# Layer 1's rows of a MetaFormer kernel: 25 depthwise taps split anew over VectorE, GpSimd and TensorE, with VectorE's sums held in PSUM

## The chip, the cores and the metric

The kernel runs as one program on one core of a Trainium2 chip. The metric is the device time of one execution in microseconds (us). Before the change three runs took 8144.84, 8158.97 and 8159.37 us; the median is 8158.97.

## The reference

Two MetaFormer layers are applied to an input of 2 images x 96 channels x 96 x 96 pixels. The change lies in the last stage of layer 1. What is computed there:

```python
lepe = lax.conv_general_dilated(v.reshape(B, C, H, W), lepe_w, (1, 1), [(pad, pad), (pad, pad)],
    dimension_numbers=('NCHW', 'OIHW', 'NCHW'), feature_group_count=C)      # 5 x 5, one filter per channel
...
dmat = jax.nn.softmax(dmat, axis=-1)               # each pixel against the 3 x 3 cells near it
feature = jnp.einsum('bnpk,bckn->bnpc', dmat, feat_unfold)
out = feature.reshape(B, hh, ww, R, R, C).transpose(0, 5, 1, 3, 2, 4).reshape(B, C, H, W)
out = out + lepe
out = jnp.einsum('oc,bchw->bohw', proj_w, out) + proj_b[None, :, None, None]
...
x = x + _L1_conv_ref(_ln_c(x), ...)
t = t + _L1_ffn_ref(_ln_t(t), ...)                 # LayerNorm, 96 -> 384 -> 96 with fp8 rounding of inputs
```

`lepe` is the part concerned: for every channel the values `v` are multiplied by 25 weights at 25 shifts ("taps") and summed.

## The kernel before

Layer 0 runs first, for both images. Layer 1 then runs image by image in three stages: `_l1_before` (normalise, keys and queries), `_l1_attention` (the result is `dist`, one vector per cell of 2 x 2 pixels), and the stage `rows`, which finishes the layer. Only `rows` is touched. It works on strips of R = 12 image rows, eight for each image, called q0 to q7 here. `_l1_turn` first turns `dist` round on TensorE. Then `_l1_rows` records for each strip:

- `values(g)`, four times: TensorE multiplies four rows of the input by `W.v` (L1694), ScalarE copies the result from PSUM into `vch` (L1697), a tile of 96 channels x 16 rows x 100 columns in fp32: the strip's 12 rows with two rows and columns around them. Small GpSimd memsets (L1681 and on) clear the edge. `vch` has three buffers.
- `near(i)`, three times: scores `st` on TensorE, exponentials `e` on ScalarE, the sums `pd` and `po` on TensorE, the inverse `rd` by Ln and Exp on ScalarE, and the product `ft` on VectorE (L1747).
- the taps. Four of the 25 (`ON_PE`) are left to TensorE. VectorE does the other 21 over the whole strip, 1152 elements of each of 96 partitions at a time: one multiplication (L1759) and 20 multiply-and-add instructions (L1762) which read `vch` and `acc` and write `acc` again, all in SBUF.
- `project(c2)` for each half of six rows, in two parts `c` of three rows (288 columns) each: TensorE sums in one bank `pp` the four taps with weights `W.pt` (L1778), `ft` times `W.p` (L1782) and, as a step of its own that waits for the taps, `acc` times `W.p` (L1788). VectorE adds bias and residual and gives `x3` (L1791). Then comes the FFN of the half, `_plan_ffn`: norm (`fxc` and `fva` on TensorE, square, Ln and Exp on ScalarE, `fxq` on VectorE, L894), `fph` on TensorE, on ScalarE six casts (L909), three Relu (L913) and three conversions to fp8 (L916) into `fh`, `fpy` on TensorE, `fy` on ScalarE (L927, L931), and the residual add on GpSimd (L932). SP issues the loads of `xn` and `xr` and the store of the half.

Single-bank PSUM tiles come from a pool `p` of eight banks.

The order in each engine's queue is not that of the code. Operations are recorded with an engine, an estimated cost, what they read and write, and a due time (`_dues`, from the last argument of `_l1_rows`; here 40 for each strip and 80 from a strip's first operation to its last). `_Plan.order` then lists them: at each step it takes an operation that can start earliest by its own estimates, the due time deciding among those ready at once, and a tile takes a buffer only when one is free. The order so found is fixed: on the chip each engine takes its queue strictly in turn, and where an operation has to wait, everything behind it in that queue waits.

Of the kernel before, what the change touches and what calls it, by code (L numbers as in the profile page):

```python
# [14 lines left out]
ALU = mybir.AluOpType  # L15
# [11 lines left out]
C = 96  # L27
HW = 96
# [5 lines left out]
H2 = T // 2  # L34
# [813 lines left out]
def _dues(S, n0, at):  # L848

    ops = S.ops[n0:]  # L850
    whole, sofar = sum(o.cost for o in ops), 0.0
    for o in ops:
        o.due = at(sofar / whole)
        sofar += o.cost
# [796 lines left out]


NEAR = 2 * (CELLS + 2)
ON_PE = tuple(range(4))


def _l1_rows(k, P, S, W, ffn, M, distT, x2, out, q, at):


    nc = k.nc  # L1660
    n0 = len(S.ops)
    R = 2 * WIN
    op = _op(S)
    ps = lambda name: S.tile(P.ps, [128, 512], "p", 8, name=name)
    temp = lambda name: S.tile(P.wk, [C, T], name, 3)
    xs = S.held(M.xs, "xs")


    vch = S.tile(P.wk, [C, R + 4, HW + 4], "vch", 3)
    y0 = q * R - 2  # L1670

    if q:
        xn = S.tile(P.wk, [C, R + 4, HW], "xn", 2)
        S.op("sp", 1.5, lambda: nc.sync.dma_start(
            xn.ap[:, : min(R + 4, HW - y0)],
            M.xd.rearrange("p (r w) -> p r w", w=HW)[:, y0 : min(y0 + R + 4, HW)]), (), (xn,))
    else:
        xn = S.held(M.xn0, "xn")

    def edges():  # L1680
        nc.gpsimd.memset(vch.ap[:, :, 0:2], 0.0)  # L1681
        nc.gpsimd.memset(vch.ap[:, :, HW + 2 :], 0.0)
        if y0 < 0:
            nc.gpsimd.memset(vch.ap[:, 0:2, :], 0.0)
        if y0 + R + 4 > HW:
            nc.gpsimd.memset(vch.ap[:, R + 2 :, :], 0.0)

    op("pool", 200, edges, (), ((vch, "e"),))

    def values(g):  # L1690
        lo, hi = max(y0 + 4 * g, 0), min(y0 + 4 * g + 4, HW)
        n = (hi - lo) * HW
        pv = ps("pv2")
        op("pe", n, lambda: nc.tensor.matmul(  # L1694
            pv.ap[:C, :n], W.v, xn.ap[:, lo - y0 : hi - y0], start=True, stop=True),
            (xn,), (pv,), (vch,))
        op("act", n, lambda: nc.scalar.copy(  # L1697
            vch.ap[:, lo - y0 : hi - y0, 2 : HW + 2],
            pv.ap[:C, :n].rearrange("p (r w) -> p r w", w=HW)), (pv,), ((vch, g),))

    for g in range(4):
        values(g)

    ft = S.tile(P.wk, [C, 3, 384], "ft", 2)

    def near(i):
        j = 3 * q + i  # L1710
        toks = slice(4 * j - y0, 4 * j - y0 + 4)
        e = [S.tile(P.wk, [NEAR, 384], "e", 4) for _ in range(2)]
        po, pd, rd = ps("po"), ps("pd"), S.tile(P.wk, [C, 384], "rd", 2)
        for t in range(2):
            st = ps("st")

            def part(t=t, st=st):
                def run():
                    nc.tensor.matmul(
                        st.ap[:NEAR, :384],  # L1720
                        xs.ap[:, 2 * j + 2 * t : 2 * j + 2 * t + 2, :].rearrange("p r w -> p (r w)"),
                        xn.ap[:, toks], start=True, stop=False)
                    nc.tensor.matmul(
                        st.ap[:NEAR, :384], W.far, W.mask[:, t], start=False, stop=True)

                op("pe", 480, run, (xs, xn), (st,), (e[t],))
                op("act", 384, lambda: nc.scalar.activation(
                    e[t].ap, st.ap[:NEAR, :384], AF.Exp, scale=C**-0.5), (st,), (e[t],), tab="e")

            part()  # L1730

        def sums(dst, w):
            def run():
                for t in range(2):
                    nc.tensor.matmul(dst.ap[:C, :384], w(t), e[t].ap, start=(t == 0), stop=(t == 1))  # L1735

            op("pe", 768, run, e + [distT], (dst,), (rd, ft))

        sums(pd, lambda t: k.ones[:NEAR])
        sums(po, lambda t: distT.ap[:NEAR, j + t])  # L1740

        def inverse():
            nc.scalar.activation(pd.ap[:C, :384], pd.ap[:C, :384], AF.Ln)
            nc.scalar.activation(rd.ap, pd.ap[:C, :384], AF.Exp, scale=-1.0)

        op("act", 384, inverse, (), (pd, rd), tab="e", times=2)
        op("dve", 384, lambda: nc.vector.tensor_tensor(  # L1747
            ft.ap[:, i], rd.ap, po.ap[:C, :384], ALU.mult), (rd, po), ((ft, i),))

    for i in range(3):  # L1750
        near(i)


    acc = S.tile(P.wk, [C, R, HW], "acc", 2)
    for n, t in enumerate(t for t in range(25) if t not in ON_PE):
        def tap(n=n, t=t):
            src = lambda: vch.ap[:, t // 5 : t // 5 + R, t % 5 : t % 5 + HW]
            if n == 0:
                S.op("dve", 0.9, lambda: nc.vector.tensor_scalar(  # L1759
                    acc.ap, src(), W.lw[:, t : t + 1], None, ALU.mult), (vch,), (acc,))  # L1760
            else:
                S.op("dve", 1.43, lambda: nc.vector.scalar_tensor_tensor(  # L1762
                    acc.ap, src(), W.lw[:, t : t + 1], acc.ap, ALU.mult, ALU.add), (vch,), (acc,))

        tap()

    def project(c2):
        xr, x3 = S.tile(P.wk, [C, T], "xr", 2), temp("x3")
        S.op("sp", 1.0, lambda: nc.sync.dma_start(
            xr.ap, x2[:, (2 * q + c2) * T : (2 * q + c2 + 1) * T]), (), (xr,))  # L1770

        def part(c):
            pp = ps("pp")
            r0, cols = c2 * WIN + 3 * c, slice(c * H2, (c + 1) * H2)

            def some():
                for n, t in enumerate(ON_PE):
                    nc.tensor.matmul(  # L1778
                        pp.ap[:C, :H2], W.pt[:, n],
                        vch.ap[:, r0 + t // 5 : r0 + t // 5 + 3, t % 5 : t % 5 + HW],  # L1780
                        start=(n == 0), stop=False)
                nc.tensor.matmul(  # L1782
                    pp.ap[:C, :H2], W.p,
                    ft.ap.rearrange("p i n -> p (i n)")[:, (2 * c2 + c) * H2 : (2 * c2 + c + 1) * H2],
                    start=False, stop=False)

            op("pe", (len(ON_PE) + 1) * H2, some, (vch, ft), (pp,))
            op("pe", H2, lambda: nc.tensor.matmul(  # L1788
                pp.ap[:C, :H2], W.p, acc.ap[:, r0 : r0 + 3, :], start=False, stop=True),
                (acc,), (pp,), (x3,))  # L1790
            op("dve", H2, lambda: nc.vector.scalar_tensor_tensor(  # L1791
                x3.ap[:, cols], pp.ap[:C, :H2], W.pb, xr.ap[:, cols], ALU.add, ALU.add),
                (pp, xr), ((x3, c),))

        for c in range(2):
            part(c)
        y = _plan_ffn(k, S, op, ps, temp, P.wk, 3, ffn, x3, True)
        row = q * R + c2 * WIN
        S.op("sp", 1.0, lambda: nc.sync.dma_start(
            out[:, row : row + WIN, :].rearrange("c r w -> c (r w)"), y.ap), (y,), ())  # L1800

    for c2 in range(2):
        project(c2)
    _dues(S, n0, at)


def _l1_turn(k, P, S, M, distT):

    nc = k.nc
    op = _op(S)  # L1810
    dist = S.held(M.dist, "dist")

    def some(g):
        pt = S.tile(P.ps, [128, 512], "p", 8, name="pt")

        def run():
            for n in range(5):
                a = 2 * (5 * g + n)
                nc.tensor.transpose(
                    pt.ap[:NEAR, n * C : (n + 1) * C],  # L1820
                    dist.ap[:, a : a + 2, :].rearrange("p r w -> p (r w)"),
                    k.ident[:C, :C])

        op("pe", 500, run, (dist,), (pt,), (distT,))
        op("act", 480, lambda: nc.scalar.copy(
            distT.ap[:NEAR, 5 * g : 5 * g + 5].rearrange("p n c -> p (n c)"), pt.ap[:NEAR, : 5 * C]),
            (pt,), ((distT, g),))

    for g in range(5):
        some(g)  # L1830
# [58 lines left out]
def _layer1(k, tc, a, x2d, out):  # L1889
    nc = k.nc  # L1890
    with ExitStack() as st:
        pool = lambda name, bufs, **kw: st.enter_context(tc.tile_pool(name=name, bufs=bufs, **kw))
        cp = pool("l1c", 1)
        W = Ctx()
        W.k, W.v, W.q = k.kvq
        ffn = None
# [13 lines left out]
        for b in range(NB):  # L1910
# [21 lines left out]
            def rows(P, S):  # L1932
                distT = S.tile(P.wk, [128, (CELLS + 2) // 2, C], "distT", 1)
                _l1_turn(k, P, S, M, distT)
                for q in range(CELLS // WIN):
                    _l1_rows(k, P, S, W, ffn, M, distT, x2d[b], out[b], q,
                             lambda v: 40.0 * q + 80.0 * v)

            with ExitStack() as st:
                plan(st, rows)  # L1940
# [106 lines left out]
```

## Time and profile before

| what | us |
| --- | --- |
| runs | 8144.84, 8158.97, 8159.37 |
| profiled execution | 8149.47 |
| its span (first to last instruction) | 8147.7 |
| stage `rows`, image 0: last step of attention to the next stage's first load | 6815 to 7143 |
| stage `rows`, image 1 | 7819 to 8147 |
| VectorE busy in the first of these (328 us) | 274.9 |
| TensorE | 293.5 |
| ScalarE | 218.4 |
| GpSimd | 33.3 |

A row of the profile gives the line of the code, the engine (PE is TensorE, PEld its weight loads, DVE VectorE, ACT ScalarE, POOL GpSimd, SP SyncE), the operation, the tiles written and read, and then count, busy time in us, mean duration in ns, and the engine's idle time just before these instructions with what ended it. Matmuls are pipelined and a wide fp32 one shows as two records of 0.41 us that follow each other every 0.24 us, so a TensorE that is shown busy isn't necessarily full. A stage's end counts in full: the next stage's first load waits for it.

### The profile page before, as it was taken

To read this page: it belongs to the slowest core of one execution; us is meant where nothing else is said; L and a number is where in the kernel's file an instruction comes from. 1 tells how busy PE (TensorE), PEld (TensorE's weight loads), DVE (VectorE), ACT (ScalarE), POOL (GpSimd) and SP (SyncE) were. 2 spreads that over 40 slices of the span, in tenths; PEclk is the share of its full clock that TensorE was granted. 3 is DMA by queue.
4 is the path that set the end of the run, shared out by engine and by line. 5 is a ranking of instruction groups with operands and counts; after the bars stand their busy time and mean duration, and the time that the engine had idled before them with its cause. 6 is when DMAs were issued, how large, how long until landed. Compare 5 with 4: busy or idle time off the path is not lost. (4 is left out here: it accounts for less than half of the span.)

```text
span 8147.7 us, 123836 instructions
## 1 busy us (share of the span) xinstructions
PE 7250.8 (89%) x46031; PEld 3210.3 (39%) x46031; DVE 7575.8 (93%) x5276; ACT 6328.2 (78%) x10672; POOL 5305.7 (65%) x3963
## 2 busy tenths in 40 slices
PE   7888888988888888898888888888878999989998
PEld 3333344444444334343443443343334224532245
DVE  3999999999999999999999999999996998869988
ACT  5788888788788887788887878887747886778867
POOL 4888888888888888888888888888861000110001
PEclk8999999999999999999999999999998999999999
DMA  3545555444545555455445554555431000110001
GB/s 94 165 157 162 159 162 162 154 155 158 163 159 161 160 160 159 155 159 160 153 155 164 160 161 157 161 162 157 154 108 47 3 2 22 32 46 3 3 23 33
DMA packets 359852, 992.23 MB, mean 122 GB/s; under 512 B 69288, under 2 KB 71680, under 8 KB 359040
## 3 DMA queue, kind: packets, MB, share of 16 engines
q1 hardware_dynamic: 357440, 984.04, 38.5%
q8 instruction: 365, 5.98, 0.3%
q14 instruction: 255, 2.09, 0.1%
q10 hardware_dynamic: 1792, 0.12, 0.0%
HBM read 797.19 MB, written 139.25 MB: 115 GB/s over the span
## 5 line engine op out<-in xcount | busy, mean ns | idle before, releaser
L1136 POOL TENSOR_TENSOR h<-h,cre 128x864 f32<-128x864 f32 x2048 | 3481.2, 1714 | 753.5 <-DVE h L1131 507.5
L1131 DVE TENSOR_TENSOR_SCAN h<-dA,bp 128x864 f32<-128x864 f32 x2048 | 3900.0, 1939 | 61.4 <-PE y L1149 39.9
L1094 ACT ACTIVATE dA<-dlr,A 128x576 f32<-128x576 f32 x3072 | 2158.7, 766 | 830.9 <-DVE h L1131 725.4
L1114 DVE TENSOR_TENSOR bp<-dur,bp 128x864 f32<-128x864 f32 x2048 | 2075.4, 1046 | 188.4 <-DMA dur<-du_d 117.3
L1149 PE MATMUL y<-h,fold 128*32 128x288 f32 (+2 forms) x18432 | 1790.0, 434 | 221.7 <-POOL h L1136 198.7
L1509 ACT ACTIVATE pr<-sc 128x960 f32<-128x960 f32 (+1 forms) x1080 | 954.1, 937 | 203.9 <-PE sc L1505 183.4
L1149 PEld LDWEIGHTS y<-h,fold 128*32 128x32 f32 x18432 | 725.9, 113 | 974.9 <-POOL h L1136 669.5
L1110 PE MATMUL bp<-bt,selb 128*128 128x288 bf16 x2048 | 613.5, 300 | 458.7 <-DVE h L1131 440.4
L1589 DVE TENSOR_TENSOR sums<-sums,pr 128x3840 f32<-128x3840 f32 (+1 forms) x240 | 959.1, 3996 | 57.0 <-ACT pr L1509 34.5
L1681 POOL MEMSET vch<- 96x32 f32 x16 | 2.4, 154 | 1321.8 <-DVE dist L1543 1211.3
L1110 PEld LDWEIGHTS <-selb 128*128 128x128 bf16 x2048 | 197.3, 96 | 1163.0 <-DVE h L1131 956.4
L1505 PE MATMUL sc<-qH,kH 32*128 32x480 f32 (+1 forms) x3240 | 627.3, 602 | 12.6 <-issue 8.0
L1505 PE MATMUL sc<-q,kH 32*128 32x480 f32 (+1 forms) x1080 | 564.8, 602 | 0.0
L1194 PE MATMUL y<-selb,minus 128*32 128x288 bf16 x3146 | 552.0, 301 | 0.0
L1571 PE MATMUL av<-pr,vT 128*32 128x480 f32 (+1 forms) x4320 | 534.1, 565 | 3.7 <-ACT av L1596 3.5
L1762 DVE SCALAR_TENSOR_TENSOR acc<-vch,lepe_w,acc 96x1152 f32<-96x1152 f32 x320 | 467.7, 1462 | 8.4 <-ACT vch L1697 0.4
L1505 PEld LDWEIGHTS sc<-qH,kH 32*128 32x128 f32 x3240 | 219.8, 184 | 422.0 <-issue 223.7
L617 PE MATMUL pc<-xin,w_ca 128*128 128x288 f32 x1152 | 366.5, 424 | 0.4 <-DVE fxq L894 0.4
L1194 PEld LDWEIGHTS <-minus 128*32 128x32 bf16 x3146 | 274.0, 100 | 212.5 <-issue 122.3
L932 POOL TENSOR_TENSOR x<-x,fy 96x576 f32<-96x576 f32 x32 | 53.2, 1662 | 461.1 <-ACT fy L931 387.7
L791 PE MATMUL pt<-xd,w_dt 96*128 96x288 f32 x768 | 264.2, 440 | 7.7 <-ACT r L797 4.8
L810 POOL TENSOR_TENSOR e<-e,du 128x576 f32<-128x576 f32 x192 | 231.5, 1206 | 31.0 <-ACT du L806 31.0
(284 smaller groups left out, 10983.1 us busy)
## 6 DMA issues: line engine op xcount, KB each, us to landing
cre<-c_d SPq DMA_DIRECT2D x1024, 288.0 KB, 3.3
dur<-du_d SPq DMA_DIRECT2D x256, 864.0 KB, 5.2
dlr<-dl_d SPq DMA_DIRECT2D x256, 864.0 KB, 5.8
x<-xs SPq DMA_DIRECT2D x512, 72.0 KB, 2.6
du_d<-du SPq DMA_DIRECT2D x128, 288.0 KB, 3.1
dl_d<-dl SPq DMA_DIRECT2D x128, 288.0 KB, 3.7
du_d<-du SPq DMA_DIRECT2D x128, 144.0 KB, 2.5
dl_d<-dl SPq DMA_DIRECT2D x128, 144.0 KB, 2.4
```

The source lines that it names most:

```text
L1094: nc.scalar.activation(dA.ap[:, :, blk, :], dlr.ap[:, blk, :].rearrange("p (c n) -> p c n", c=2), AF.Exp, scale=k.A[:, i, kg, h, blk : blk ...
L1110: nc.tensor.matmul(bp.ap[:, :H2], k.selb[:, kk, i, :], f.bc[o].ap[:, toks], start=True, stop=True)
L1114: nc.vector.tensor_tensor(bp.ap[:, : NBL * H2].rearrange("p (b n) -> p b n", b=NBL)[:, ::-1], dur.ap[:, ::-1, toks], bp.ap[:, :H2].unsquee ...
L1131: nc.vector.tensor_tensor_scan(hv, dv, bv, 0.0, ALU.mult, ALU.add)
L1136: nc.gpsimd.tensor_tensor(ht.ap, ht.ap, cre.ap[:, toks].unsqueeze(1).to_broadcast([128, NBL, H2]), ALU.mult)
L1149: nc.tensor.matmul(dst, k.fold, v, start=start, stop=stop)
L1194: nc.tensor.matmul(P.awake.ap[NBL * CB :, T - HEAD + 2 * 72 : HEAD], k.minus[:, :CB], k.selb[:, 0].rearrange("p i m -> p (i m)")[:, : HEAD ...
L1505: nc.tensor.matmul(two[to // 2][:, to % 2, :n], kH[rows, k0 : k0 + 128], q, start=True, stop=True)
L1509: nc.scalar.activation(pr[:, 2 * i : 2 * i + 2, :n], two[i][:, :, :n], AF.Exp, scale=HD**-0.5)
L1571: nc.tensor.matmul((main if s < HEADS else other)[s * HD : (s + 1) * HD, :n], vT[:, blk, hd, :], pr[:, place(s, p), :n], start=at == 0, st ...
L1589: nc.vector.tensor_tensor(both, both, pr[:, :, :, :n], ALU.add)
L1762: S.op("dve", 1.43, lambda: nc.vector.scalar_tensor_tensor(acc.ap, src(), W.lw[:, t : t + 1], acc.ap, ALU.mult, ALU.add), (vch,), (acc,))
```

## The change

- Taps: one (`ON_PE`) stays on TensorE, five (`ON_POOL`) go to GpSimd, 19 are left to VectorE.
- GpSimd makes each of its taps as a product of `vch` and a weight spread over the strip, into `pacc` (the first) or `one`, and adds each later product to `pacc`: five products and four sums. `pacc` and `one` have two buffers each, in SBUF.
- VectorE's sum lies in `accp`, 3 PSUM banks with 384 columns of each used. Its first tap reads `vch` and `pacc` and writes `accp`; the next 17 read `vch` and `accp` and write `accp`; the last writes `acc` in SBUF.
- `accp` takes three banks, and the pool `p` has five in place of eight.
- The four rows that a strip shares with the one before are copied by GpSimd from the old `vch` in place of `values(0)`, from q1 on.
- A part of `project` is one TensorE step that waits for `acc` as a whole, with three products (tap, `ft`, `acc`) in place of six.
- Due times: 32 for each strip and 64 across one, for 40 and 80; a tap's estimated cost for VectorE is 1.35, a GpSimd operation's 2.4.

```diff
-ON_PE = tuple(range(4))
+ON_PE = (2,)
+ON_POOL = (0, 1, 5, 6, 10)
...
-    ps = lambda name: S.tile(P.ps, [128, 512], "p", 8, name=name)
+    ps = lambda name: S.tile(P.ps, [128, 512], "p", 5, name=name)
...
-    for g in range(4):
+    if last is None:
+        values(0)
+    else:
+        op("pool", 4 * HW, lambda: nc.gpsimd.tensor_copy(vch.ap[:, 0:4, :], last.ap[:, R:, :]),
+           ((last, 3), (last, "e")), ((vch, 0), (vch, "e")))
+    for g in range(1, 4):
         values(g)
...
-    acc = S.tile(P.wk, [C, R, HW], "acc", 2)
-    for n, t in enumerate(t for t in range(25) if t not in ON_PE):
-        def tap(n=n, t=t):
-            src = lambda: vch.ap[:, t // 5 : t // 5 + R, t % 5 : t % 5 + HW]
-            if n == 0:
-                S.op("dve", 0.9, lambda: nc.vector.tensor_scalar(
-                    acc.ap, src(), W.lw[:, t : t + 1], None, ALU.mult), (vch,), (acc,))
-            else:
-                S.op("dve", 1.43, lambda: nc.vector.scalar_tensor_tensor(
-                    acc.ap, src(), W.lw[:, t : t + 1], acc.ap, ALU.mult, ALU.add), (vch,), (acc,))
-
-        tap()
+    near_acc = S.tile(P.wk, [C, R, HW], "pacc", 2, skip=2)
+    sums_p, acc = S.tile(P.ps, [128, 3, 512], "accp", 1), S.tile(P.wk, [C, R, HW], "acc", 2)
+    tap = lambda t: vch.ap[:, t // 5 : t // 5 + R, t % 5 : t % 5 + HW]
+
+    def pooled(n, t):
+        dst = S.tile(P.wk, [C, R, HW], "one", 2, skip=0) if n else near_acc
+        S.op("pool", 2.4, lambda: nc.gpsimd.tensor_tensor(
+            dst.ap, tap(t), W.lw[:, t : t + 1].unsqueeze(2).to_broadcast([C, R, HW]), ALU.mult),
+            (vch,), (dst,))
+        if n:
+            S.op("pool", 2.4, lambda: nc.gpsimd.tensor_tensor(
+                near_acc.ap, near_acc.ap, dst.ap, ALU.add), (dst,), (near_acc,))
+
+    def summed(n, t, end):
+        rows3 = lambda v: v.rearrange("p (a r) w -> p a r w", a=3)
+        part = lambda: sums_p.ap[:C, :, : 4 * HW].rearrange("p a (r w) -> p a r w", w=HW)
+        r, w = (sums_p if n else near_acc), (acc if end else sums_p)
+        S.op("dve", 1.35, lambda: nc.vector.scalar_tensor_tensor(
+            rows3(acc.ap) if end else part(), rows3(tap(t)), W.lw[:, t : t + 1],
+            part() if n else rows3(near_acc.ap), ALU.mult, ALU.add), (vch, r), (w,))
+
+    for n, t in enumerate(ON_POOL):
+        pooled(n, t)
+    rest = [t for t in range(25) if t not in ON_PE + ON_POOL]
+    for n, t in enumerate(rest):
+        summed(n, t, t == rest[-1])
...
-            op("pe", (len(ON_PE) + 1) * H2, some, (vch, ft), (pp,))
-            op("pe", H2, lambda: nc.tensor.matmul(
-                pp.ap[:C, :H2], W.p, acc.ap[:, r0 : r0 + 3, :], start=False, stop=True),
-                (acc,), (pp,), (x3,))
+                nc.tensor.matmul(
+                    pp.ap[:C, :H2], W.p, acc.ap[:, r0 : r0 + 3, :], start=False, stop=True)
+
+            op("pe", (len(ON_PE) + 2) * H2, some, (vch, ft, acc), (pp,), (x3,))
...
+                last = None
                 for q in range(CELLS // WIN):
-                    _l1_rows(k, P, S, W, ffn, M, distT, x2d[b], out[b], q,
-                             lambda v: 40.0 * q + 80.0 * v)
+                    last = _l1_rows(k, P, S, W, ffn, M, distT, x2d[b], out[b], q, last,
+                                    lambda v: 32.0 * q + 64.0 * v)
```

The listing finds another order. Three stretches of queues of the built program, the same for both images, shortened to strip, half and tile:

```text
VectorE: ... last tap q2 | x3 q1.1, fxq q1.0 x2, ft q2, x3 q1.1, fxq q1.1 x2, x3 q2.0 x2, ft q3 x2,
         x3 q2.1, fxq q2.0 | first tap q3 ...
ScalarE: ... FFN q1.0 (6 casts, 3 Relu, 3 fp8), squares q1.1 x2, copies to vch q3 x3, fy q1.0, Ln/Exp q1.1 x2,
         e x4, FFN q1.1, rd x2, fy q1.1, ...
GpSimd:  ... add (L932) q0.0, q0.1, memsets q4, product q3, product q3, add q1.0, sum, product, sum,
         product, sum, product, add q1.1, sum (pacc of q3 is complete) ...
```

In the old order no more than two operations other than taps stand between two strips' taps on VectorE.

More of the change, by code (lines that the diff above doesn't have):

```diff
@@ L1653, with _l1_rows @@
 NEAR = 2 * (CELLS + 2)
-ON_PE = tuple(range(4))
-def _l1_rows(k, P, S, W, ffn, M, distT, x2, out, q, at):
+ON_PE = (2,)
+ON_POOL = (0, 1, 5, 6, 10)
+def _l1_rows(k, P, S, W, ffn, M, distT, x2, out, q, last, at):
     nc = k.nc
@@ L1804, in _l1_rows @@
     _dues(S, n0, at)
+    return vch
 def _l1_turn(k, P, S, M, distT):
@@ L1813, in some @@
     def some(g):
-        pt = S.tile(P.ps, [128, 512], "p", 8, name="pt")
+        pt = S.tile(P.ps, [128, 512], "p", 5, name="pt")
         def run():
```

## The prediction

> **What bounds the kernel now.** I looked first at the busy shares in slices to find where the changed code runs: only in two stages, 6815 to 7143 us (image 0) and 7819 to 8147 us (image 1). Then at busy time by stretch (us, then busy time of each engine, granted clock, DMA):
>
> ```profile
> 6815.00:6824.00 9.00, 8.29 (x33) 6.32 (x34) 0.82 (x2) 4.07 (x8) 2.88 (x8) 0.50 0.76 182
> 6960.00:6995.00 35.00, 32.29 (x126) 18.49 (x125) 34.54 (x33) 24.35 (x54) 3.10 (x4) 1.00 0.16 43
> 7104.00:7143.00 39.00, 20.48 (x78) 11.66 (x76) 4.89 (x11) 30.50 (x64) 5.08 (x4) 0.65 0.08 23
> ```
>
> In mid-stage VectorE (third) is busy 34.54 of 35 us, TensorE (first) 32.29, ScalarE (fourth) 24.35, GpSimd (last) 3.10. A stage is thus a head of 9 us, 280 us at VectorE's pace (35 us for each of eight strips q0 to q7), and a tail of 39 us at ScalarE's. The groups of instructions of that stage say what VectorE does (count, busy, mean ns, idle before):
>
> ```profile
> L1762 DVE SCALAR_TENSOR_TENSOR acc<-vch,lepe_w,acc 96x1152 f32<-96x1152 f32 x160 | 234.5, 1466 | 4.4 <-ACT vch L1697 0.4
> L1791 DVE SCALAR_TENSOR_TENSOR x<-pp,proj_b,xr 96x288 f32<-96x288 f32 x32 | 15.9, 507 | 6.5 <-PE pp L1788 6.5
> L894 DVE TENSOR_TENSOR fxq<-fxc,frs 96x288 fp8e5<-96x288 f32 x32 | 13.7, 446 | 16.3 <-ACT frs L863 16.3
> L1747 DVE TENSOR_TENSOR ft<-rd,po 96x384 f32<-96x384 f32 x24 | 12.8, 544 | 4.1 <-PE po L1735 4.1
> L1759 DVE TENSOR_SCALAR acc<-vch,lepe_w 96x1152 f32<-96x1152 f32 x8 | 6.5, 809 | 8.2 <-DMA xn<-xd 8.2
> ```
>
> Taps are 241 of its 283 us. They never wait for another engine (4.4 us idle over 160), since their input `vch` is there strips ahead. Last, waits and the timeline:
>
> ```profile
> POOL x L932 <- DVE acc L1762: 43.4, 3, 15.4
> 6842.61 15.91 DVE L1762 SCALAR_TENSOR_TENSOR acc<-vch,lepe_w,acc 96x1152 f32<-96x1152 f32 x11
> ```
>
> Eleven dependent taps in 15.91 us: one every (15.91-1.41)/10 = 1.45 us.
>
> [...] taps of 1399 ns at least reach 2500, and GpSimd's add L932 has a mean of 1682 ns here against 1279 in layer 0. [...] its sum arrives through SBUF and a strip's first new tap still has two SBUF inputs. [...]
>
> **The change, part by part.** Prices from these page rows:
>
> ```profile
> L1136 POOL TENSOR_TENSOR h<-h,cre 128x864 f32<-128x864 f32 x2048 | 3481.2, 1714 | 753.5 <-DVE h L1131 507.5
> L1114 DVE TENSOR_TENSOR bp<-dur,bp 128x864 f32<-128x864 f32 x2048 | 2075.4, 1046 | 188.4 <-DMA dur<-du_d 117.3
> L810 POOL TENSOR_TENSOR e<-e,du 128x576 f32<-128x576 f32 x192 | 231.5, 1206 | 31.0 <-ACT du L806 31.0
> ```
>
> *VectorE's tap.* [...] 1.39 us; every 1.43 in a dependent chain. Ends: 1.36 and 1.47 (no gain). I take 1.435. Per strip 18 x 1.435 + 1.40 = 27.2 us for 19 taps, against 20 taps at 1.45, the first at 0.81, and some 0.9 of exclusion: 30.7. Saved: 3.5 us a strip, 28 a stage.
>
> *GpSimd's nine operations* per strip (five products, four sums). L810 to L1136 rises 508 ns in 288 elements: 1714+508 = 2.22 us at 1152, with 0.05 between them 2.27; nine take 20.4 us. With two adds L932 (1.28), memsets and the copy some 24 us: less than VectorE's strip, so GpSimd doesn't bound by its sum. [...]
>
> *TensorE* loses 12 matmuls a strip of 0.49 us (pairs of 0.24), 47 us a stage, and `values(0)` seven times; ScalarE 7 x 0.48. Both were beside VectorE: nothing gained, but TensorE no longer presses.
>
> *What is added to the path.* The first tap of a strip now waits for that strip's nine GpSimd operations (`pacc`), these for the whole of `vch`. Where this bites I read from the order of the built program, which gives each engine's queue; times are then laid along it with durations of the trace. Call F the first tap of a strip, A the end of its last.
>
> Head: `vch` is full at 6824.9 (ScalarE's last copy, 6824.44+0.48), so F(q0) = 6824.9+20.4 = 6845.4, where the old taps began at 6823.7; VectorE has only five `ft` products (2.7 us) meanwhile. GpSimd then runs ahead: A(q0) = 6872.6, A(q1) = 6902.4 (19 taps, 4 `x3`, an `ft`), A(q2) = 6933.6 (19 taps, 4 `fxq`, 2 `x3`, 1 `ft`).
>
> Then a hole. In the new order VectorE has, after the last tap of q2, thirteen small operations (5 `x3`, 5 `fxq`, 3 `ft`, 6.4 us) before the first tap of q3. The reason: TensorE's `values` of q3 stand behind the FFN norm of q1's second half, whose `x3` VectorE runs only after q2's taps. From A(q2): `x3`, `fxq` twice, `ft`, `x3`, in lockstep with ScalarE's Ln/Exp, 5.5 us; then ScalarE's queue has the FFN of q1's first half (six casts, three Relu, three fp8: 6 x 0.34 + 3 x 1.46 = 6.4), two squares 0.8, three copies to `vch` 1.4: with gaps 14.4 us. GpSimd starts there: nine operations 20.4 and two L932, which stand between them, 2.6. F(q3) = A(q2)+37.4 = 6971.0. VectorE loses 31 us. Even with a faster GpSimd the order holds it some 34 us, because q2's own first `fxq` stands ahead of F(q3) and waits behind q1's second FFN half on ScalarE.
>
> A(q3) = 7000.6 (19 taps, 2.4 of others). q4's `vch` is copied at about F(q3)+11.9 (q2's FFN half 8-9 us, squares, three copies), then 20.4+1.3: F(q4) = 7004.6, a loss of 2.5. A(q4) = 7034.7. q5's last copy to `vch` stands behind both FFN halves of q3 on ScalarE; the second's `fxq` comes after twelve taps of q4: F(q4)+18.7, +9 for this FFN, then 20.4+1.3 on GpSimd: F(q5) = 7054 against A(q4) = 7034.7 and 4 us of other work: 15.5 lost. q6 and q7 have their sums in time: A(q5) = 7082.2, A(q6) = 7114.9, A(q7) = 7146.7.
>
> Tail: the old last tap ended at 7104.2, the next stage's first DMA was issued at 7142.9: 38.7. Three FFN halves on ScalarE set it in both orders; that the two other matmuls of each `pp` part now wait for `acc` (about 1 us a part) is hidden by the first of these. New end 7185.4: 42.5 later, as the sum says too: head +21.7 for what GpSimd does alone, holes +49, taps -28. The order is the same for image 1. The profiled execution took 8149.5 (span 8147.7 and 1.8 around it), so 8149.5+85 = 8235. The median of the runs is 9.5 higher at 8159.0, from 8144.8 to 8159.4; I forecast on the profiled one's basis and leave that difference to the range.
>
> Smaller edits. Five instead of eight single PSUM banks: within the holes they are in the times above; elsewhere 0 to 2 us a strip (cover: taps that VectorE has in store), taken 0. First taps colliding with GpSimd: 0 to 1.5 us each, taken 0. Three weights fewer in `W.pt` and SP's queue (same DMAs, a little moved): nothing; transfers have landed long before (DMA share 0.16).
>
> **Rivals.**
> - *The holes close* (ends faster): GpSimd stays ahead after q0. For it: its sum of 24 us per strip is less than 31. Against: the order. Without the 49 us a stage is 6.5 shorter: 8136. It decides where the loss in holes falls below 42 us a stage.
> - *Only q3's hole is real*: q5's copies come earlier than laid out, as ScalarE has slack then. Saves 15.5+2 a stage: 8200.
> - *Five banks bind in every strip*: a norm holds up to four banks across a round of three engines. 2 us in each of eight strips, 16 a stage: 8267.
>
> **How the numbers follow.** Holes as laid out 68% (own range 8200 to 8270: GpSimd's operation on 36 places a stage, -10 to +9; taps +-7; handovers +-6), only q3's 12%, banks 12%, holes closed 8%. Range 8185 to 8285. A measurement of this kernel can't tell 0.2% (16 us) from no change; the last case, 13 us faster, lies near that bound and is split, with an edge of the second added to "same": slower 0.90, same 0.05, faster 0.05.
>
> **What would show it.** Taps of about 1.40 us without 2.5 us outliers; GpSimd operations of 2.2; VectorE idle 18 to 20 us at the stage's start, some 30 between q2 and q3 and 15 between q4 and q5, released by GpSimd; stages of 365 to 375 us. I am wrong if VectorE is busy over 95% between first and last tap, or if GpSimd's products take half as long.

## The result, and the profile after

The changed kernel takes 8242.11 us (median of six runs, 8239.15 to 8249.44) beside 8158.66 for the kernel before on the same chip: a ratio of 1.0104, 95% interval 1.0092 to 1.0115, 83 us slower. Its profiled execution took 8244.07 us. The forecast was 8235 (8185 to 8285).

In all that follows a stage runs from the end of `dist` to the next stage's first load, for image 0. It grew from 327.3 to 367.4 us, and image 1's by 40.0. To within 4 us these 80 are the difference of the two medians.

First the busy times by stretch in the changed kernel (us, then busy time of TensorE, its weight loads, VectorE, ScalarE and GpSimd, granted clock, DMA share, GB/s). The stretches are the head, the hole between q2 and q3, a stretch at full pace and the tail:

```profile
6829.00:6864.00 35.00, 34.33 (x119) 19.95 (x120) 3.05 (x6) 18.15 (x36) 28.66 (x21) 0.87 0.26 65
6953.00:6989.00 36.00, 31.87 (x121) 17.67 (x122) 6.55 (x14) 29.29 (x64) 23.58 (x15) 1.00 0.17 46
7085.00:7120.00 35.00, 26.81 (x94) 14.15 (x93) 34.51 (x32) 20.89 (x46) 33.27 (x17) 0.92 0.06 19
7161.00:7197.00 36.00, 19.03 (x72) 10.18 (x72) 4.42 (x10) 27.33 (x57) 3.81 (x3) 0.71 0.06 19
```

The third column is the story. VectorE is as full as before at 7085, but it did 3 us of work in the first 35 and 6.5 us in the 36 after q2. Before the change it began 8 us into the stage and had no hole.

The groups of VectorE's instructions in that stage (count, then busy us, mean ns, idle time before and what ended it):

```profile
L1777 DVE SCALAR_TENSOR_TENSOR accp<-vch,lepe_w,accp 96x1152 f32<-96x1152 f32 x136 | 192.7, 1417 | 3.7
L1810 DVE SCALAR_TENSOR_TENSOR x<-pp,proj_b,xr 96x288 f32<-96x288 f32 x32 | 16.2, 510 | 33.0 <-PE pp L1806 32.9
L894 DVE TENSOR_TENSOR fxq<-fxc,frs 96x288 fp8e5<-96x288 f32 x32 | 13.9, 448 | 24.6 <-ACT frs L863 24.6
L1777 DVE SCALAR_TENSOR_TENSOR accp<-vch,lepe_w,pacc 96x1152 f32<-96x1152 f32 x8 | 13.9, 1732 | 0.4 <-POOL pacc L1770 0.4
L1753 DVE TENSOR_TENSOR ft<-rd,po 96x384 f32<-96x384 f32 x24 | 13.0, 546 | 37.4 <-PE po L1741 37.4
```

Taps wait for nothing: 3.7 and 0.4 us. The idle time stands before the small operations: 33.0 before `x3` (6.5 before the change), 24.6 before `fxq` (16.3), 37.4 before `ft` (4.1). By place, 32.0 of it (all before `ft`) lie in the head; 26.5 before `x3` and 13.7 before `fxq` lie between the first tap and the last, where the order puts these operations between two strips' taps; 17.4 before the two lie in the tail, which had 20.5 before the change. A row that is cheap by its busy time can still be where the stage waits.

The hole between q2 and q3 on VectorE's timeline (start us, duration us, in brackets the idle time just before and its releaser):

```profile
6951.47 1.41 DVE L1777 SCALAR_TENSOR_TENSOR acc<-vch,lepe_w,accp 96x1152 f32<-96x1152 f32 x1
...
6969.19 0.45 DVE L894 TENSOR_TENSOR fxq<-fxc,frs 96x288 fp8e5<-96x288 f32 x1 [10.02 <-ACT frs L863]
6969.99 0.45 DVE L894 TENSOR_TENSOR fxq<-fxc,frs 96x288 fp8e5<-96x288 f32 x1 [0.35 <-ACT frs L863]
6977.95 0.51 DVE L1810 SCALAR_TENSOR_TENSOR x<-pp,proj_b,xr 96x288 f32<-96x288 f32 x1 [7.51 <-PE pp L1806]
...
6987.27 0.52 DVE L1810 SCALAR_TENSOR_TENSOR x<-pp,proj_b,xr 96x288 f32<-96x288 f32 x1 [3.97 <-PE pp L1806]
6987.71 0.44 DVE L894 TENSOR_TENSOR fxq<-fxc,frs 96x288 fp8e5<-96x288 f32 x1
6988.55 1.65 DVE L1777 SCALAR_TENSOR_TENSOR accp<-vch,lepe_w,pacc 96x1152 f32<-96x1152 f32 x1 [0.40 <-POOL pacc L1770]
```

And on GpSimd's timeline over the same time:

```profile
6966.69 2.10 POOL L1766 TENSOR_TENSOR pacc<-vch,lepe_w 96x1152 f32<-96x1152 f32 x1 [8.80 <-ACT vch L1698]
6968.76 2.12 POOL L1766 TENSOR_TENSOR one<-vch,lepe_w 96x1152 f32<-96x1152 f32 x1
...
6986.30 2.22 POOL L1770 TENSOR_TENSOR pacc<-pacc,one 96x1152 f32<-96x1152 f32 x1
```

From q2's last tap (6951.47 + 1.41 = 6952.88) to q3's first (6988.55) is 35.7 us, with 6.2 of work. Two chains run side by side and end within 0.4 us of each other: GpSimd's nine operations, from q3's copies to `vch` to 6988.5, and VectorE's own small operations, which wait for `frs` and `pp` and end at 6988.15. So shortening either alone would not have closed this hole, and a table of waits that names a releaser sees only the later one.

In the two smaller holes it is VectorE's own chain that ends last. Before q4 GpSimd's sum was ready at 7020.45 and the first tap started at 7023.60. Before q5, VectorE and then GpSimd:

```profile
7070.38 0.51 DVE L1810 SCALAR_TENSOR_TENSOR x<-pp,proj_b,xr 96x288 f32<-96x288 f32 x1 [2.03 <-PE pp L1806]
7070.82 1.41 DVE L1777 SCALAR_TENSOR_TENSOR accp<-vch,lepe_w,pacc 96x1152 f32<-96x1152 f32 x1
```

```profile
7067.66 2.22 POOL L1770 TENSOR_TENSOR pacc<-pacc,one 96x1152 f32<-96x1152 f32 x1
```

GpSimd was 0.9 us early there; the tap stood behind an `x3` that waited for TensorE's `pp`.

The head on VectorE's timeline:

```profile
6845.55 0.55 DVE L1753 TENSOR_TENSOR ft<-rd,po 96x384 f32<-96x384 f32 x1 [16.03 <-PE po L1741]
...
6863.67 0.55 DVE L1753 TENSOR_TENSOR ft<-rd,po 96x384 f32<-96x384 f32 x1 [5.92 <-PE po L1741]
6864.15 1.44 DVE L1777 SCALAR_TENSOR_TENSOR accp<-vch,lepe_w,pacc 96x1152 f32<-96x1152 f32 x1
6865.62 24.68 DVE L1777 SCALAR_TENSOR_TENSOR accp<-vch,lepe_w,accp 96x1152 f32<-96x1152 f32 x17
```

GpSimd had its first sum ready at 6857.3. The first tap waited on to 6864.15, since the fifth `ft` stands ahead of it in the queue and waits for TensorE.

### The profile page after: what moved, and what is told of

It is laid out like the page before. It is cut to its first block, busy times and chain, and to the rows that moved or that the text cites. A ratio compares the mean times of both kernels' runs of the same rounds, so it can differ in the third digit from the quotient of the medians.

```text
span 8242.3 us, 123135 instructions
## 1 busy us (share of the span) xinstructions
PE 7216.4 (88%) x45619; PEld 3165.0 (38%) x45619; DVE 7535.7 (91%) x5241; ACT 6325.4 (77%) x10658; POOL 5609.7 (68%) x4121
## 5 line engine op out<-in xcount | busy, mean ns | idle before, releaser
L1114 DVE TENSOR_TENSOR bp<-dur,bp 128x864 f32<-128x864 f32 x2048 | 2077.2, 1047 | 202.0 <-DMA dur<-du_d 119.9
L1589 DVE TENSOR_TENSOR sums<-sums,pr 128x3840 f32<-128x3840 f32 (+1 forms) x240 | 959.0, 3996 | 55.6 <-ACT pr L1509 33.5
L1777 DVE SCALAR_TENSOR_TENSOR accp<-vch,lepe_w,accp 96x1152 f32<-96x1152 f32 x272 | 385.3, 1417 | 7.3
L617 PEld LDWEIGHTS pc<-xin,w_ca 128*128 128x128 f32 x1152 | 194.6, 191 | 142.0 <-issue 98.8
```

The costliest lines, as they stand in the source:

```text
L1114: nc.vector.tensor_tensor(bp.ap[:, : NBL * H2].rearrange("p (b n) -> p b n", b=NBL)[:, ::-1], dur.ap[:, ::-1, toks], bp.ap[:, :H2].unsquee ...
L1589: nc.vector.tensor_tensor(both, both, pr[:, :, :, :n], ALU.add)
L1777: S.op("dve", 1.35, lambda: nc.vector.scalar_tensor_tensor(rows3(acc.ap) if end else part(), rows3(tap(t)), W.lw[:, t : t + 1], part() if ...
```

## The experiments

All of them at a glance: the median, the ratio to the kernel before on the same chip with its interval, and image 0's stage, split at the end of the last tap. The stage is that of one profiled execution, which lay 16 us above the median in tensor32 and 14 below it in headearly32.

| run | us | ratio (95%) | stage | to last tap | tail |
| --- | --- | --- | --- | --- | --- |
| before | 8158.66 | 1 | 327.3 | 288.6 | 38.7 |
| after | 8242.11 | 1.0104 (1.0092 to 1.0115) | 367.4 | 331.3 | 36.1 |
| early | 8207.68 | 1.0066 (1.0050 to 1.0083) | 348.2 | 282.7 | 65.5 |
| sbuf5 | 8396.55 | 1.0295 (1.0278 to 1.0312) | 445.9 | 409.2 | 36.6 |
| sbuf8 | 8394.56 | 1.0294 (1.0276 to 1.0311) | 442.4 | 407.9 | 34.5 |
| psum_only | 8209.64 | 1.0065 (1.0048 to 1.0082) | 352.3 | 306.4 | 46.0 |
| before5 | 8238.26 | 1.0099 (1.0079 to 1.0119) | 365.1 | 319.5 | 45.6 |
| merge5 | 8243.70 | 1.0113 (1.0098 to 1.0128) | 372.1 | 324.7 | 47.4 |
| seven | 8189.62 | 1.0035 (1.0024 to 1.0046) | 339.7 | 305.5 | 34.2 |
| tensor | 8168.16 | 1.0010 (1.0003 to 1.0017) | 328.0 | 280.9 | 47.2 |
| tensor16 | 8157.23 | 1.0002 (0.9994 to 1.0010) | 328.3 | 273.1 | 55.2 |
| tensor32 | 8162.94 | 1.0009 (1.0001 to 1.0018) | 328.9 | 249.5 | 79.4 |
| headearly32 | 8184.49 | 1.0028 (1.0018 to 1.0038) | 337.0 | 276.5 | 60.6 |
| copy5 | 8154.78 | 0.9990 (0.9983 to 0.9997) | 322.8 | 283.9 | 38.8 |

### What is the sum in PSUM worth? (sbuf5, sbuf8)

The changed kernel with VectorE's sum put back into SBUF, once with five banks in `p` (each engine's queue in the changed kernel's order) and once with eight (an order without long stretches between taps):

```diff
-    sums_p, acc = S.tile(P.ps, [128, 3, 512], "accp", 1), S.tile(P.wk, [C, R, HW], "acc", 2)
+    acc = S.tile(P.wk, [C, R, HW], "acc", 2)
...
+        r = acc if n else near_acc
+            acc.ap, tap(t), W.lw[:, t : t + 1], r.ap, ALU.mult, ALU.add), (vch, r), (acc,))
```

> The changed kernel with VectorE's sum in SBUF (acc) instead of the three PSUM banks; five single banks as in the change, and the same order of all queues. Theory (two SBUF inputs of a tap and GpSimd's operations shut each other out): some 50 of GpSimd's 72 operations a stage run beside taps and cost VectorE 0.8 (the share of the add L932 in the kernel before) to 2.2 us each: 80 to 220 us in all, 8320 to 8460. Rival (putting the sum in PSUM brings nothing[...]): 8242 within 15.

> The same as the last, but with eight single PSUM banks. The order found with eight banks has no stretch of small operations between strips. Theory A (the holes come from the order, and the order from the three banks taken away): the waits of q3 and q5 are gone, so it is some 90 us faster than the run with the sum in SBUF and five banks, less what more overlap costs in exclusion (20 to 60): 30 to 70 us faster. Theory B (GpSimd's lateness doesn't depend on banks): VectorE still waits 30 us before q3, the same time within 20.

The group of taps in the stage of sbuf5, then that of sbuf8:

```profile
L1775 DVE SCALAR_TENSOR_TENSOR acc<-vch,lepe_w,acc 96x1152 f32<-96x1152 f32 x144 | 284.9, 1979 | 4.0
```

```profile
L1775 DVE SCALAR_TENSOR_TENSOR acc<-vch,lepe_w,acc 96x1152 f32<-96x1152 f32 x144 | 314.7, 2185 | 3.9
```

In the same queue order the same 144 taps take 1979 ns on average in place of 1417: 144 x 0.562 = 81 us a stage, and the run is 154 us longer for two stages. The theory held. The median tap of sbuf5 is still 1415 ns; the longest is 3266, for 1420 in the changed kernel. The 53 multiply-and-add taps that overlap one of GpSimd's nine operations average 2905 ns, the other 99 average 1452; in the changed kernel it is 1451 and 1418. So the taps aren't slower in SBUF, they are held while GpSimd works, and GpSimd is held by them: a strip's first product rises from 2.10 to 2.66 us on average, a sum from 2.22 to 2.86. This is what "exclusion" stands for here: a tap with both inputs in SBUF and a GpSimd operation that run side by side both take longer, by these amounts. sbuf8 adds that eight banks and an order without long holes (36 us before q3 in sbuf5, 5.4 here) give nothing (2 us) while the exclusion lasts: more GpSimd work falls beside taps, 74 of them in place of 53, and the group above now averages 2185. Its time is that of theory B, but the holes went as theory A had it; what they gave was lost to exclusion. Without the sum in PSUM, GpSimd's share of the taps would have cost some 240 us.

### What do the three banks cost? (psum_only, before5, merge5)

psum_only is the kernel before with nothing changed but VectorE's 21 taps summed in `accp` and five banks left. before5 has only the five banks; three lie idle. merge5 is before5 with the one-step `project` part of the changed kernel.

```diff
-    ps = lambda name: S.tile(P.ps, [128, 512], "p", 8, name=name)
+    ps = lambda name: S.tile(P.ps, [128, 512], "p", 5, name=name)
...
-        pt = S.tile(P.ps, [128, 512], "p", 8, name="pt")
+        pt = S.tile(P.ps, [128, 512], "p", 5, name="pt")
```

> The kernel before with only VectorE's sum moved to three PSUM banks (21 taps, the first as a plain product into PSUM; five single banks; four taps on TensorE, nothing new on GpSimd). Theory: a tap every 1.435 us for 1.448 (-2 us a stage), no exclusion by GpSimd's adds (-7.5), the first tap 1.40 for 0.81 (+5): -9 us in all, about 8150 (8140 to 8162). Rival (five banks bind): TensorE at 93% busy stalls, 2 us a strip, about 8190.

> The kernel before with one edit: the pool of single PSUM banks has five in place of eight; three banks lie idle. Theory (five banks bind: the 54 us that the sum in PSUM alone cost came from the banks): 8199 us (8185 to 8212), that run less 16 first taps by 0.6 us; VectorE idle before x3 for TensorE's pp by 25 us or more a stage, against 6.5. Rival (the taps' place in PSUM cost it, the banks are free as I took them): 8145 to 8165.

> The kernel before with five banks (8238), and with a part of project as one TensorE step that waits for acc as a whole, as in the changed kernel. Theory (three banks cost so much because a part begun early holds its bank until the taps are done; the one step, a part of the change that I costed at nothing, takes most of that away): 8185 (8165 to 8210). Rival (five banks cost what they cost by the FFNs and the scores alone, the step changes nothing): 8225 to 8250.

VectorE's rows in the stage of psum_only:

```profile
L1766 DVE SCALAR_TENSOR_TENSOR accp<-vch,lepe_w,accp 96x1152 f32<-96x1152 f32 x152 | 215.2, 1416 | 4.0
L1797 DVE SCALAR_TENSOR_TENSOR x<-pp,proj_b,xr 96x288 f32<-96x288 f32 x32 | 16.1, 510 | 36.8 <-PE pp L1794 26.6 <-issue 10.3
L1762 DVE TENSOR_SCALAR accp<-vch,lepe_w 96x1152 f32<-96x1152 f32 x8 | 11.3, 1412 | 7.7 <-DMA xr<-x2d 7.5
```

And in that of before5:

```profile
L1762 DVE SCALAR_TENSOR_TENSOR acc<-vch,lepe_w,acc 96x1152 f32<-96x1152 f32 x160 | 231.4, 1446 | 4.6
L1791 DVE SCALAR_TENSOR_TENSOR x<-pp,proj_b,xr 96x288 f32<-96x288 f32 x32 | 16.3, 511 | 46.5 <-PE pp L1788 37.8 <-issue 8.4
```

before5 costs 77 us (8238.26 beside 8161.29), above what I expected and close to what the whole change lost. The place is the row of `x3`: 46.5 us idle where the kernel before had 6.5, 40 us a stage; 37.8 of the 46.5 end with TensorE's `pp`. The edit is five banks, but the queues differ too: for five banks the listing finds another order, with up to four small operations between two strips' taps on VectorE. So the 77 us are the price of the banks with that order; how much the same order would take with eight banks was not run. psum_only costs 54, more than either expectation; it is cheaper than before5 though its first taps cost more (1412 ns for 809), as its taps don't collide with GpSimd (1416 ns on average for 1446) and `x3` waits 10 us less, again in an order of its own. So with the same five banks the time moves by 23 us. merge5 takes nothing away (8243.70, as its rival had it): that a part begun early holds its bank was not it.

### Do the banks make the holes? (seven)

A sum of three banks beside seven others would take ten, and the kernels here use at most eight. So this twin leaves the sum out: a tap reads one bank of zeros three times over and writes SBUF. Its operands are of the changed kernel's kind (one input in SBUF, one in PSUM, 1152 elements); `p` has seven banks.

```diff
-        part = lambda: sums_p.ap[:C, :, : 4 * HW].rearrange("p a (r w) -> p a r w", w=HW)
+        part = lambda: sums_p.ap[:C, : 4 * HW].rearrange("p (r w) -> p r w", w=HW).unsqueeze(1).to_broadcast([C, 3, 4, HW])
...
-            rows3(acc.ap) if end else part(), rows3(tap(t)), W.lw[:, t : t + 1],
+            rows3(acc.ap), rows3(tap(t)), W.lw[:, t : t + 1],
```

> A twin of the changed kernel for the timing of its banks: VectorE's taps read one PSUM bank of zeros, three times over, in place of the sum so far, and write acc in SBUF; the sum of VectorE's taps is so left out of the output, but each tap still has one input in SBUF and one in PSUM and 1152 elements. The sum takes one bank in place of three and the pool p has seven in place of five; all else (GpSimd's nine operations, the first tap's wait for them, copied rows, the one step of a part, due times) is the changed kernel's. Theory (three banks cause the loss, by holding back the FFNs and the values and so making the holes): head as in the changed kernel 34.6, eight strips of 27.3 for taps, some 33 of other work, tail 38: 324 a stage against 368, so 8242 - 88 = 8154 (8140 to 8180). Rival (the first tap's wait for GpSimd makes the holes whatever the banks): 8210 to 8250.

The passage from q2 to q3 on its VectorE timeline:

```profile
6949.44 1.41 DVE L1777 SCALAR_TENSOR_TENSOR acc<-vch,lepe_w,accp 96x1152 f32<-96x1152 f32 x1
...
6955.34 0.55 DVE L1753 TENSOR_TENSOR ft<-rd,po 96x384 f32<-96x384 f32 x1 [0.85 <-PE po L1741]
6955.81 1.41 DVE L1777 SCALAR_TENSOR_TENSOR acc<-vch,lepe_w,pacc 96x1152 f32<-96x1152 f32 x1
```

The hole of 35.7 us is 5.0 (6949.44 + 1.41 to 6955.81), with GpSimd doing the same nine operations ahead of every strip. The stage is 27.7 us shorter and the run 52 us: between the two expectations, nearer the theory. Of the 40 us that the stage had lost, then, some 28 hang on the two banks, together with the order that the listing finds for seven: the two were not taken apart. What stays is 339.7 against 327.3. The head adds 27.8: the first tap starts 36.0 us after `dist` (34.6 in the changed kernel, 8.2 before). From there to the last tap it is 11.0 shorter than before the change, with smaller holes left in it (12.1 us before q7), and the tail 4.5 shorter.

### What does the wait for GpSimd cost? (tensor)

GpSimd's sum goes to TensorE as one more product of a part; VectorE's first tap is a plain product into PSUM and waits for no GpSimd. Five banks stay. The planned order changes with it.

```diff
-        r, w = (sums_p if n else near_acc), (acc if end else sums_p)
+        if not n:
+            S.op("dve", 1.35, lambda: nc.vector.tensor_scalar(
+                part(), rows3(tap(t)), W.lw[:, t : t + 1], None, ALU.mult), (vch,), (sums_p,))
+            return
...
+                nc.tensor.matmul(
+                    pp.ap[:C, :H2], W.p, near_acc.ap[:, r0 : r0 + 3, :], start=False, stop=False)
```

> The changed kernel, but GpSimd's sum goes to TensorE as one more product of a part, and VectorE's first tap is a plain product into PSUM: VectorE never waits for GpSimd, five banks stay, and the planned order has no long stretch without taps between two strips. Theory (five banks and the wait for GpSimd add up): the kernel with PSUM sums alone took 8210; two taps fewer on VectorE are 2 x 1.45 x 16 = 46 us, so 8164 (8145 to 8180), below the changed kernel by 60 or more. Rival (five banks alone hold the pace, whatever VectorE has to do): 8200 to 8240.

8168.16, as the theory had it: 74 us below the changed kernel with the same five banks. The head is back at 8.2 us. Of the loss of 83 us two more banks remove 52 and no wait for GpSimd 74: the two gains overlap and can't be added. In the order of the changed kernel this wait ends last ahead of q3 alone, by 0.4 us, so the 74 us are not its price by itself: they come with another order, and the two were not taken apart. One account fits both runs, though none isolates it: with five banks a strip's `vch` comes late, and in the changed kernel 22 us of GpSimd stand behind it, alongside the small operations that the order puts there. VectorE's timeline shows what late values cost without GpSimd behind them, at the first taps of q4 and q5:

```profile
6969.61 1.42 DVE L1777 TENSOR_SCALAR accp<-vch,lepe_w 96x1152 f32<-96x1152 f32 x1 [5.86 <-issue]
...
7006.76 1.42 DVE L1777 TENSOR_SCALAR accp<-vch,lepe_w 96x1152 f32<-96x1152 f32 x1 [5.86 <-issue]
```

5.86 us a strip. "issue" says that the profile shows no releaser; GpSimd's first product of the strip, which needs the same tile, starts 0.06 us later (7006.82) and is released by ScalarE's copies to `vch`.

### Can a better order win it back? (early, headearly32, tensor16, tensor32)

Each shifts the due times of a strip's loads, edges, values and GpSimd taps ahead, by 64 in early and by the number in the other names. In headearly32 q0 also leaves no taps to GpSimd. tensor16 and tensor32 start from tensor.

```diff
     _dues(S, n0, at)
+    for o in ahead:
+        o.due -= 64.0
```

> The changed kernel; the due times of each strip's load, edges, values and GpSimd taps are 64 earlier, so only the order of the queues differs: in the new VectorE queue at most two or three small operations stand between the last tap of a strip and the first of the next. Theory (the loss is the queue order: vch of q3 and q5 comes late, GpSimd's nine operations follow it, VectorE waits some 46 us a stage, and 7 us at the head behind the products ft): 8242 - 92 - 13, about 8137 (8120 to 8160), VectorE over 95% busy between the first and the last tap. Rival (GpSimd's work or five PSUM banks bind in every strip): the waits come back elsewhere, 8200 or more.

> The changed kernel with two edits: strip q0 leaves no taps to GpSimd (its VectorE does 24), and loads, edges, values and GpSimd's taps of each strip are due 32 earlier (64 in the run before, where the tail grew by what the holes gave). Theory (holes, head and tail are one budget of order; a mean shift keeps the holes shut and lets the FFNs follow their strips): head -18, holes -45, five more taps +7, tail +5 a stage at most: 8242 - 2 x 50 = 8140 (8130 to 8175). Rival (with five banks the FFNs on TensorE and ScalarE set the pace, so what VectorE gains comes back as a tail): 8195 to 8215, as the shift by 64 alone gave.

> GpSimd's sum to TensorE as in the run named tensor (8168), and each strip's loads, edges, values and GpSimd taps due 16 earlier. In that run's trace the first tap of q4 to q7 waited 5.86 us each for its strip's values, whose copies stood behind an FFN half on ScalarE. Theory (late values are all that is left between strips, and a small shift leaves the FFNs where they were): 8168 - 2 x 23.4 = 8121 (8110 to 8150), faster than the kernel before. Rival (five banks: what the values gain the FFNs lose, and it comes back as a tail): 8155 to 8190.

> The same with a shift of 32. Its planned order ends with four FFN halves and more behind the last tap, against three halves with 16. Theory: the values come no better than with 16, the tail is one half longer (some 9 us a stage): 8140 (8125 to 8165), above the run with 16. Rival: 8155 to 8190, as with 16.

In early the holes before q3 to q5 go (10 us of idle time before q6 and q7 stay), and the head is 8.2 us shorter, though GpSimd's sum and the third `ft`, which end within 0.6 us of each other, still keep the first tap 26.4 us from `dist`. The last tap ends 48.6 us sooner. Yet the run gains 34 us in place of 105, a time that only the rival allowed. Its VectorE timeline, after the last tap (ended at 7108.61):

```profile
7117.27 0.45 DVE L894 TENSOR_TENSOR fxq<-fxc,frs 96x288 fp8e5<-96x288 f32 x1 [4.52 <-ACT frs L863]
...
7135.47 0.45 DVE L894 TENSOR_TENSOR fxq<-fxc,frs 96x288 fp8e5<-96x288 f32 x1 [7.18 <-ACT frs L863]
...
7147.12 0.45 DVE L894 TENSOR_TENSOR fxq<-fxc,frs 96x288 fp8e5<-96x288 f32 x1 [5.76 <-ACT frs L863]
...
7160.23 0.45 DVE L894 TENSOR_TENSOR fxq<-fxc,frs 96x288 fp8e5<-96x288 f32 x1 [5.49 <-ACT frs L863]
```

VectorE ran ahead and the FFNs lagged: the tail is 65.5 us for 36.1. headearly32 fits neither expectation: 55 us gained to the last tap, 24 given back in the tail. tensor16 took the time of its rival, tensor32 one that both its expectations allow. With tensor these two show it best. Busy times by stretch, split at the last tap's end, of tensor, tensor16 and tensor32 in turn:

```profile
6830.00:7111.00 281.00, 246.63 (x886) 136.99 (x887) 242.81 (x229) 183.13 (x387) 178.34 (x111) 0.93 0.14 36
7111.00:7159.00 48.00, 28.55 (x101) 15.76 (x100) 5.85 (x13) 36.79 (x77) 5.08 (x4) 0.73 0.08 23
```

```profile
6816.00:7089.00 273.00, 240.79 (x859) 135.88 (x860) 243.74 (x226) 176.99 (x377) 178.09 (x111) 0.91 0.14 37
7089.00:7145.00 56.00, 36.84 (x130) 20.72 (x128) 7.44 (x16) 40.75 (x87) 5.43 (x5) 0.74 0.08 24
```

```profile
6839.00:7089.00 250.00, 219.62 (x779) 121.16 (x779) 239.48 (x220) 157.57 (x336) 161.01 (x102) 0.92 0.14 37
7089.00:7169.00 80.00, 57.32 (x211) 32.35 (x209) 10.25 (x22) 60.99 (x128) 22.82 (x14) 0.82 0.09 25
```

VectorE is done after 281, 273 and 250 us, and in the last it is 96% busy on the way; the stage takes 328.0, 328.3 and 328.9. ScalarE's share of the tail rises from 36.8 to 61.0 us of work. A VectorE that is 31 us faster is worth nothing here. What holds the 328 us, banks, the order of the queues or the lockstep of the FFN between three engines, isn't settled: neither TensorE (shown busy 275 of 328 us in tensor) nor ScalarE (220) is full.

### One tap less without GpSimd (copy5)

The kernel before with the shared rows copied and five taps on TensorE, so 20 on VectorE; sums in SBUF, eight banks.

```diff
-ON_PE = tuple(range(4))
+ON_PE = tuple(range(5))
```

> The kernel before (sums in SBUF, eight banks, nothing on GpSimd but the copy) with the shared rows copied and five taps on TensorE, 20 on VectorE. Theory (VectorE's taps set the pace and TensorE has room once the shared rows are copied): one tap fewer in 16 strips by 1.45 us = 23, so 8132 (8122 to 8145). Rival (TensorE presses: four more matmuls a strip by 0.49 us, and it is shown busy for 293 of 328 us): 8155 to 8180.

8154.78, at the edge of the rival's range: 6.5 us below the kernel before on the same chip, where 23 were hoped for. It is the only run whose interval lies below the kernel before, by 0.1% (0.03 to 0.17%).

## Why the prediction was right, and where it was not

The sign and the places came out as laid out along the new order: a stage 40.1 us longer where 42.5 were forecast, lost in the head and in the three holes, over what the taps gave. That the total is so near is in part luck: the head was 4.8 us above its forecast, holes, taps and tail 3.0, 1.8 and 2.6 below. And what ended the waits was mostly not what the prediction named: GpSimd's sum came last before q3 alone, by 0.4 us. The base was the profiled execution, 9 us below the median: 85 us of change were forecast, 83 measured.

- **Taps.** Forecast -28 a stage. Measured from first to last tap, less the three holes: 296.7 - 46.0 - 280.5 = -29.8, of which 2.7 are `ft` products that moved to the head. The price of one was off: 1417 ns and one every 1.454 us (24.68 us for 17), no better than in SBUF, where I took 1.39 and 1.435. The gain was an estimate from two other instructions of the trace before. L1589, on pairs in SBUF, takes 4156 ns at 3840 elements and 3356 at 3072, 1.042 ns an element, which leaves 156 ns that don't grow with the size. L1114, in place in PSUM, takes 1046 ns at 864 elements, which at the same rate leaves 146. That is a gain of 10 ns; the forecast had 24, from 4170 in place of 4156. Even 10 did not carry over to this instruction. The first tap of a strip, taken at 1.40, averages 1.73: collisions with GpSimd, which I had put at 0, up to 3.44 us (q1, while two GpSimd operations ran from 6892.13 to 6897.5, the second in 3.22 us for 2.10). Together some 5 us a stage, made up by the idle time between taps outside the holes, which fell by some 7.
- **GpSimd's operation.** 2.22 for a sum, as forecast; a free product takes 2.10. Nine in q0 took 19.6 us (20.4).
- **Head.** Forecast +21.7, measured +26.5 (34.6 for 8.2). The step that failed is "VectorE has only five `ft` products (2.7 us) meanwhile": counted as work and not as waits. They stand ahead of the first tap and the last of them comes 6.4 us after GpSimd's sum. That sum was itself 2 us earlier than forecast (27.8 after `dist` for 29.8), by the faster operations and because GpSimd starts before `vch` is full: its first product at 6837.74, ScalarE's last copy at 6838.37. The tap of that product doesn't read the last four rows.
- **Holes.** Forecast 31 + 2.5 + 15.5 = 49; measured idle 29.4 + 3.4 + 13.1 = 46.0. The layout along the built order, with durations from the trace before, carried the forecast. For q3 I also said that the order would hold it some 34 us even with a faster GpSimd; both chains ended within 0.4 us. For q4 and q5 the layout had GpSimd's sum as the last to come, and it was 3.2 and 0.9 us ahead of the first tap: there the sizes came out near because the other chain was about as long, which the prediction did not weigh. So "released by GpSimd" was wrong as a sign to look for: only 0.4 us has that name. A sum was off as well: with the terms given, A(q2) is 6932.9 and not 6933.6, which makes the forecast 0.7 us a stage too long.
- **Tail.** Forecast 38.7, measured 36.1.
- **Five banks.** "Taken 0" outside the holes held in the changed kernel, where the strips without a hole wait 0.4 us each; the rival of 2 us in every strip did not come. But the text put the holes down to the order and left open what made the order. seven and before5 show that it is in good part the banks, by way of the order that the listing finds for their number. The rival in which only q3's hole is real fell with the 13.1 us before q5.
- **The rival in which the holes close** was priced at 8136 with an unchanged tail. early closed most of them and took 8208: that price was wrong by the FFNs, the second limit behind VectorE, which the prediction did not weigh for a faster VectorE.
- **The rest of the time.** Layer 0, which the change doesn't touch, took 12 us more in this profiled execution; the medians differ by 83 where the two stages give 80.

## What to carry to other kernels

Moving taps from VectorE to GpSimd had three prices, not two: what the operations cost, what exclusion costs, and what the room that avoids it costs. The operations themselves were worth some 54 us over the two stages, exclusion would have cost 154 us in the same order, and taking three PSUM banks from the kernel before cost 77 us by itself. The room was paid for in the order of the queues, and so it showed up where a strip's taps wait behind small operations (46.5 us idle before `x3` in before5 for 6.5). Before paying to shorten the busiest engine, look for what would end the stage without it: where the time up to its last tap shrinks and the tail grows by the same (from tensor to tensor32 280.9 to 249.5 and 47.2 to 79.4 us), that engine is no longer the bound.

## What the runs showed of the hardware

- Multiply-and-add over 96 x 1152 fp32 takes 1419 ns with sum and result in PSUM (changed kernel) and 1415 in SBUF (kernel before), both medians, and comes every 1.45 us in both. The last tap of a strip, which adds a sum in PSUM and writes SBUF, takes 1410 ns.
- A plain product by a per-partition weight is another matter: 809 ns into SBUF (kernel before), 1412 into PSUM (psum_only), 603 ns more for the same 1152 elements.
- Exclusion between VectorE and GpSimd stretches both (sbuf5): a tap with both inputs in SBUF from 1415 ns to as much as 3266, a strip's first GpSimd product from 2.10 to 2.66 us on average. With the sum in PSUM the longest tap that reads it took 1420 ns (changed kernel).
- GpSimd multiplies 96 x 1152 elements by a weight spread over them in 2.10 us, faster than it adds two such tiles in place (2.22; both in the changed kernel).
